# When stored sets give back their slots, and where a new set's square is issued, in a fused two-layer convolution kernel

## The chip, the cores and the metric

The kernel runs on one core of a Trainium2 chip. The metric is the device time of one execution in microseconds (us), lower is better. Before the change, three runs took 9905.83, 9907.52 and 9934.52 us; their median, 9907.52 us, is the time before.

## The reference, cut to what matters

The input x has 8 elements of 8 channels of 512 x 512, all float32. Layer 0 adds a small spectral convolution to x. Layer 1 takes the group-normalised result (called `xn` in the kernel) and runs three parts on it:

```python
drive = grid = x                       # a coupled map lattice, 15 steps
for _ in range(15):
    mapped = 3.9 * grid * (1.0 - grid)
    local = conv3x3_per_channel(mapped, K_local)
    physics = 0.7 * mapped + 0.3 * local
    grid = 0.85 * physics + 0.15 * drive
cml_out = clip(grid, 0.0001, 0.9999)
h = relu(conv3x3(x, Wp) + bp)          # 8 -> 128 channels
nca_out = sigmoid(conv1x1(h, Wu) + bu) # 128 -> 8
gin = concat([x, cml_out, nca_out])
g = sigmoid(conv1x1(relu(conv3x3(gin, Wg1))))
out = x + g * cml_out + (1 - g) * nca_out
```

The change touches the book-keeping of the lattice part alone. It does not change what is computed.

## The kernel before, in words

**The work.** Every element goes through four kinds of work, and one instruction stream per engine mixes them by hand: the lattice (`Half`, `convolve`, `settle`), the hidden convolution (`Hidden`: matmuls at L636, relus at L642 on ScalarE and L644 on VectorE, the 1x1 convolution at L655), the gate of the element before (`Gate`, L706 and L723), and the spectral layer of the element after (`layer0`: L305, L313, L363, L401 with its copy `ty` at L405, L433).

**The lattice.** Each element has two halves of four channels (`first`, `second`). A half is cut into five sets, k = 0 to 4, each four slabs of 32 rows. A set needs three tiles of 128 x 4 x 512: `dE` and `dO`, the drive for the even and the odd steps, loaded from `xn` by four DMAs of 256 KB each (L494), and `m`, the state. The first state is the square of `dE` minus a half: a MEMSET of two border columns on GpSimd (L515) and one ACTIVATE on ScalarE (L516), both in `square(k)`. A set's step is 48 matmuls in float32 (L536; the profile shows 96 records), two VectorE operations that take the result out of PSUM and add the drive (L591), and two squares on ScalarE (L597). A drive is scaled on GpSimd in `drive` (L529).

**The order.** A *tick* (`work`, L892) does two set-steps, A then B. An element has 75 ticks: ticks 0 to 37 hold the first half's 75 set-steps and the first one of the second half (tick 37 is A = first half, k = 4, step 15, and B = second half, k = 0, step 1), ticks 38 to 74 the rest. Step 15 of the first half is in ticks 35 (k = 0, 1), 36 (k = 2, 3) and 37 (k = 4); that of the second half is in ticks 72 (B, k = 0), 73 (k = 1, 2) and 74 (k = 3, 4). I call ticks 35 to 39 the *middle turn* (eight of them, one in each element) and ticks 72 to 76 the *end turn* (seven: ticks 75 and 76 are ticks 0 and 1 of the next element). In a tick, every engine gets its instructions in this order: the drives that are due (`prepare`), convolve A, convolve B with A's `settle`, the loads (`transfers`, which calls `others.feed` and then `fetch`), up to two rounds of the hidden convolution with their relus, the rest of B's `settle`, `squares()` (L906), then gate or spectral work and the 1x1 convolution, whose result gets its sigmoid on ScalarE every second time (L668), then `tick()` (L915), which issues what was put off to the end of this tick: the stores and the exchange of border rows (`renew`). All the DMAs named here are issued on SyncE's queue (SP), which handles them one after the other.

**The slots.** The tiles of sets live in a pool of 15 slots, `sets`, handed out first in, first out: `take` pops the oldest free slot, `drop` appends one. A half holds all 15 until its step 14. Then `settle` drops `dE` at step 14 and `dO` at step 15 (L603), and `m` after its store: `leave` (L568) clips the state on VectorE (L571) and puts off to the end of the tick a function that issues four DMAs to `cml` (L577) and drops the slot (L581). The half that comes next takes them: `fetch` (L509) loads its drives in the order (k, dE), (k, dO) for k = 0 to 4 as long as a slot is free, in each tick from eleven set-steps ahead on; `squares(n)` (L504) makes the state of set k in the tick in which k - 2 is n or n + 1, n being the half's own count, which makes it the tick before the set's first step. So `square` asks for a slot without asking whether one is free; and a slot that is handed out while its last user's store is still under way makes its new user wait for that store.

Of the kernel before, what the change touches and what calls it, by code (L numbers as in the profile page):

```python
# [128 lines left out]
def conv_layers(ctx: ExitStack, tc: tile.TileContext, a, out):  # L129
# [27 lines left out]
    sets, shared = Slots("set", 15), Slots("shared", SHARED)  # L157
# [12 lines left out]
    def later(ticks, work):  # L170
        put_off.append((now[0] + ticks, work))

    def tick(end=False):
        now[0] += 1
        due = [w for at, w in put_off if end or at <= now[0]]
        put_off[:] = [] if end else [(at, w) for at, w in put_off if at > now[0]]
        for work in due:
            work()
# [296 lines left out]
    class Half:  # L475
# [27 lines left out]

        def squares(self, n):  # L504
            for k in range(SETS):
                if k - 2 in (n, n + 1):
                    self.square(k)

        def fetch(self, n):  # L509
# [21 lines left out]
    def convolve(m, c0, step, ps):  # L531
        for n, dx in enumerate((1, 0, 2)):
            for t in range(4):
                for h in range(4):
                    at = slice(32 * h, 32 * h + 32)
                    nc.tensor.matmul(  # L536
                        ps[h // 2][32 * t : 32 * t + 32, h % 2],
                        band[at, c0 + (t if step % 2 else h), dx],
                        m[at, t, dx : dx + N],
                        start=(n == 0), stop=(n == 2), tile_position=(32 * h, 32 * t),  # L540
                    )
# [26 lines left out]
    def leave(m, k, half):  # L568

        g = m[:, :, 1 : N + 1]  # L570
        nc.vector.tensor_scalar(g, g, 0.0001, 1.0 - 0.0001, ALU.max, ALU.min)  # L571

        def store():
            for h in range(4):
                s = 4 * k + h
                lo, hi = SHARES[s]
                nc.sync.dma_start(  # L577
                    out=half.cml[1 + STARTS[s] + lo : 1 + STARTS[s] + hi, half.c0 : half.c0 + 4],
                    in_=g[32 * h + lo : 32 * h + hi],
                )  # L580
            sets.drop(m)  # L581

        later(1, store)

    def settle(half, step, k, ps):

        m, d = half.m[k], half.d[k, step % 2]
        u = m[:, :, 1 : N + 1]
        for q in range(2):
            at = slice(2 * q, 2 * q + 2)  # L590
            nc.vector.scalar_tensor_tensor(  # L591
                u[:, at], ps[q], FLOOR, d[:, at], ALU.max, ALU.add
            )
            if q:
                yield
            if step < STEPS:
                nc.scalar.square(u[:, at], u[:, at])  # L597
        if step == 1:
            half.drive(k, 0)
        elif step == STEPS - 2:  # L600
            nc.gpsimd.tensor_scalar(d, d, 0.5, None, ALU.add)  # L601
        elif step >= STEPS - 1:
            sets.drop(d)  # L603
        if step == STEPS:
            leave(m, k, half)
        elif (step - k) % HALO == 0:
            later(1, lambda: renew(half.m, k, step))
# [284 lines left out]
    def work(sets, rounds, e, after, transfers, squares=lambda: None):  # L892

        settled = iter(())
        for (half, step, k), ps in zip(sets, (pairs[:2], pairs[2:])):
            convolve(half.m[k], half.c0, step - 1, ps)
            next(settled, None)
            settled = settle(half, step, k, ps)
            next(settled)
            others.finish()  # L900
        others.finish()
        transfers()
        for ps in (pairs[:2], pairs[2:])[:rounds]:
            e.hidden.round(ps, after, settled)
        next(settled, None)
        squares()  # L906

        a, b, c, d = (pairs[i] for i in ((0, 1, 3, 2), (2, 0, 3, 2))[rounds == 1])

        point = rounds and e.hidden.n % 2 == 0  # L910
        others.first([a, b if point else c])
        if point:
            e.hidden.point(c[:, 0])
        others.second([d if point else c])
        tick()  # L915

    elements = [e]
    for n in range(-FIRST_ROUNDS, 0, 2):
# [2 lines left out]
    for b in range(B):  # L921
# [6 lines left out]
        for t in range(TICKS):  # L928
            assert not after or t < TICKS - 5 or not after.pieces
            halves = [(e.first, 2 * t), (e.second, 2 * t - TICKS)]  # L930
            if after:
                halves.append((after.first, 2 * t - 2 * TICKS))
            for half, n in halves:
                half.prepare(n)

            def squares():
                for half, n in halves:
                    half.squares(n)

            def transfers():  # L940
                others.feed(t)
                for half, n in halves:
                    half.fetch(n)

            now_sets = []
            for n in (2 * t, 2 * t + 1):
                half = (e.first, e.second)[n // TICKS]
                now_sets.append((half, n % TICKS // SETS + 1, n % SETS))

            more = done + (t + 1) * (rounds - done) // TICKS - e.hidden.n  # L950
            work(now_sets, min(more, 2 - e.hidden.n % 2), e, after and after.hidden, transfers, squares)
# [66 lines left out]
```

## Time and profile before

| what | value |
|---|---|
| median of three runs | 9907.52 us |
| the profiled execution's own time | 9903.73 us |
| its span, first to last instruction | 9901.9 us |
| around the span | 1.8 us |
| mean granted TensorE clock | 0.988 |
| TensorE (PE) busy | 9355.4 us, 94% of the span |
| VectorE (DVE) busy | 5876.2 us, 59% |
| ScalarE (ACT) busy | 4301.9 us, 43% |
| GpSimd (POOL) busy | 1762.5 us, 18% |
| DMA packets of the data queue q1 | 51.3% of 16 engines' span |

The trace is one profiled execution. A row of a timeline reads: start in us from the span's start, duration, engine, line, operation, what it writes and reads, how many were merged into the row, and in brackets how long the engine was idle before it and what ended that. "PEld" is the weight load. "issue" as a releaser means that no wait explains the idle time. A row of the waits reads: engine and line that waited, what it waited for, then us in total, times, longest. Several such waits may pass at once on different engines, and only those that TensorE feels at 94% busy can move the end of the kernel.

Where TensorE's lattice matmuls (L536) are counted off in groups of 192, a group begins each tick; in that way ticks are placed in the trace below.

### The profile page before, as it was taken

What the parts mean: (1) busy time and instruction counts of PE and PEld (TensorE: products, weight loads), DVE (VectorE), ACT (ScalarE), POOL (GpSimd) and SP (SyncE); (2) the same over time, 40 slices, a digit from 0 to 9 for tenths busy, and PEclk for the clock granted to TensorE, in tenths of its full rate; (3) what the DMA queues carried; (4) which work ended last, traced back from release to release, by engine and by line L of the source; (5) the groups of instructions that cost most, each with busy time, mean ns of one, the idle gap of its engine ahead of it and who ended that gap; (6) DMA issues with size and microseconds to landing.
All of it is one profiled execution on the core that took longest, in us unless ns stands there. A gap on an engine that the chain in (4) does not pass through costs nothing. (4 is left out here: it accounts for less than half of the span.)

```text
span 9901.9 us, 353033 instructions
## 1 busy us (share of the span) xinstructions
PE 9355.4 (94%) x160496; PEld 4299.0 (43%) x160496; DVE 5876.2 (59%) x6067; ACT 4301.9 (43%) x4445; POOL 1762.5 (18%) x1406
## 2 busy tenths in 40 slices
PE   6999999999999999999999999999999999898999
PEld 3444444444444434444344444444434444444433
DVE  5665555665566655666556655566555665555655
ACT  2544444443444434444444444445444454344423
POOL 2010111103121131111312013120221202221212
PEclk9999999999999999999999999999999999999999
DMA  5241355446544465445655356652665525753688
GB/s 152 86 121 34 80 141 135 138 126 167 139 129 142 129 162 138 133 128 136 163 140 143 117 141 162 145 157 94 148 164 139 161 97 142 171 124 95 147 200 202
DMA packets 625130, 1353.61 MB, mean 137 GB/s; under 512 B 72570, under 2 KB 72698, under 8 KB 593618
## 3 DMA queue, kind: packets, MB, share of 16 engines
q1 hardware_dynamic: 621280, 1329.89, 51.3%
q8 instruction: 1261, 20.66, 0.9%
q14 instruction: 235, 1.93, 0.1%
q10 hardware_dynamic: 2354, 1.14, 0.0%
HBM read 992.42 MB, written 268.78 MB: 127 GB/s over the span
## 5 line engine op out<-in xcount | busy, mean ns | idle before, releaser
L536 PE MATMUL pair<-m,band 32*32 32x512 f32 x115200 | 4093.8, 605 | 212.5 <-issue 99.6
L597 ACT ACTIVATE m<-m 128x1024 f32<-128x1024 f32 x2240 | 2363.7, 1055 | 2812.8 <-DVE m L591 2685.0
L536 PEld LDWEIGHTS pair<-m,band 32*32 32x32 f32 x115200 | 2258.3, 103 | 1955.8 <-issue 983.1
L636 PE MATMUL pair<-cols,w_p 32*128 32x511 f32 (+1 forms) x24576 | 2862.1, 603 | 47.0 <-issue 15.9
L591 DVE SCALAR_TENSOR_TENSOR m<-pair,dO 128x1024 f32<-128x1024 f32 x1280 | 1506.5, 1219 | 1384.6 <-PE pair L536 1214.6
L636 PEld LDWEIGHTS pair<-cols,w_p 32*128 32x128 f32 x24576 | 1275.9, 186 | 1645.0 <-issue 1116.1
L591 DVE SCALAR_TENSOR_TENSOR m<-pair,dE 128x1024 f32<-128x1024 f32 x1120 | 1318.8, 1219 | 1075.4 <-PE pair L536 870.9
L644 DVE TENSOR_SCALAR h<-pair,b_p 128x1024 f32<-128x1024 f32 x1024 | 1313.0, 1283 | 812.1 <-PE pair L636 803.3
L642 ACT ACTIVATE h<-pair,b_p 128x1024 f32<-128x1024 f32 x1024 | 1141.4, 1115 | 1044.1 <-PE pair L636 1043.9
L655 PE MATMUL pair<-h,w_u 128*32 128x512 f32 x8192 | 995.0, 598 | 136.2 <-DVE h L644 124.7
L729 POOL TENSOR_TENSOR mix<-mix 96x512 f32<-96x512 f32 x344 | 438.0, 1273 | 3809.0 <-ACT mix L727 3598.7
L706 PE MATMUL pair<-gin,w_g 128*32 128x511 f32 (+1 forms) x8256 | 965.9, 601 | 31.1 <-DMA gin<-nca 17.0
L711 POOL TENSOR_TENSOR mix<-mix 96x512 f32<-96x512 f32 x344 | 446.9, 1299 | 2006.1 <-DMA mix<-nca 1276.1
L601 POOL TENSOR_SCALAR dO<-dO 128x2048 f32<-128x2048 f32 x80 | 431.9, 5411 | 1228.5 <-DVE m L591 1228.5
L655 PEld LDWEIGHTS pair<-h,w_u 128*32 128x32 f32 x8192 | 249.0, 110 | 756.7 <-issue 384.7
L706 PEld LDWEIGHTS pair<-gin,w_g 128*32 128x32 f32 x8256 | 235.8, 110 | 711.3 <-issue 471.6
L668 ACT ACTIVATE y<-y,b_u 128x512 f32<-128x512 f32 x256 | 184.7, 721 | 808.5 <-DVE y L664 808.3
L734 DVE SCALAR_TENSOR_TENSOR mix<-mix,back 96x512 f32<-96x512 f32 x344 | 327.0, 951 | 147.3 <-POOL mix L729 147.3
L662 ACT COPY y<-pair 128x512 f32<-128x512 f32 x256 | 149.8, 585 | 599.8 <-PE pair L655 490.3
L716 DVE TENSOR_SCALAR mix<-pair,b_g 128x512 f32<-128x512 f32 x344 | 257.9, 750 | 247.8 <-PE pair L706 247.8
L723 PE MATMUL pair<-mix,w_g 128*32 128x512 f32 x2064 | 356.5, 593 | 10.5 <-DVE mix L716 8.5
L529 POOL TENSOR_SCALAR dO<-dO,base 128x512 f32<-128x512 f32 x320 | 238.6, 763 | 437.1 <-DMA dO<-xn 246.3
(86 smaller groups left out, 2661.4 us busy)
## 6 DMA issues: line engine op xcount, KB each, us to landing
gin<-xn SPq DMA_DIRECT2D x344, 384.0 KB
cols<-xn SPq DMA_DIRECT2D x256, 512.0 KB
x<-in_x SPq DMA_DIRECT2D x120, 1024.0 KB
gin<-cml SPq DMA_DIRECT2D x344, 320.0 KB
gin<-nca SPq DMA_DIRECT2D x344, 320.0 KB
dE<-xn SPq DMA_DIRECT2D x320, 256.0 KB
dO<-xn SPq DMA_DIRECT2D x320, 256.0 KB
mix<-xn SPq DMA_DIRECT2D x344, 192.0 KB
```

What stands on the lines that cost most here:

```text
L536: nc.tensor.matmul(ps[h // 2][32 * t : 32 * t + 32, h % 2], band[at, c0 + (t if step % 2 else h), dx], m[at, t, dx : dx + N], start=(n == ...
L591: nc.vector.scalar_tensor_tensor(u[:, at], ps[q], FLOOR, d[:, at], ALU.max, ALU.add)
L597: nc.scalar.square(u[:, at], u[:, at])
L601: nc.gpsimd.tensor_scalar(d, d, 0.5, None, ALU.add)
L636: nc.tensor.matmul(ps[g // 2][:, g % 2, lo:hi], w_p[p, dx, i % 2], self.cols[p, i // 2, at : at + hi - lo], start=(n == 0), stop=(n == 2), ...
L642: nc.scalar.activation(h[:, :2], ps[0], AF.Relu, bias=b_p)
L644: nc.vector.tensor_scalar(h[:, 2:], ps[1], b_p, 0.0, ALU.add, ALU.max)
L655: nc.tensor.matmul(ps[32 * g : 32 * g + 32], w_u[:, r % 4], h[:, g], start=(r == self.hs[0][0]), stop=(r == self.hs[-1][0]), tile_position ...
L706: nc.tensor.matmul(ps[32 * j : 32 * j + 32, lo:hi], gband[:, dx], gin[:, j, at : at + hi - lo], start=(n == 0), stop=(n == 2), tile_positi ...
L711: nc.gpsimd.tensor_tensor(d, d, ng, ALU.subtract)
L723: nc.tensor.matmul(ps[at], gpoint[:, at], mix[:, 3], start=True, stop=True, tile_position=(0, 32 * j),)
L729: nc.gpsimd.tensor_tensor(d, d, mix[: GR * C, 2], ALU.mult)
```

## The change

`leave` no longer drops the slot of a stored state in the function that issues the stores; that function puts the drop off once more, to the end of the next tick. `squares` makes a set's square only if it is not there yet and if a slot is free. And `work` calls `squares()` a second time at its very end, behind `tick()`. So what found no slot behind the relus is made at the tick's end, after the slots whose turn has come were given back.

```diff
@@ -503,7 +503,7 @@
 
         def squares(self, n):
             for k in range(SETS):
-                if k - 2 in (n, n + 1):
+                if k - 2 in (n, n + 1) and k not in self.m and sets.free:
                     self.square(k)
 
@@ -578,7 +578,7 @@
                     out=half.cml[1 + STARTS[s] + lo : 1 + STARTS[s] + hi, half.c0 : half.c0 + 4],
                     in_=g[32 * h + lo : 32 * h + hi],
                 )
-            sets.drop(m)
+            later(1, lambda: sets.drop(m))
 
         later(1, store)
 
@@ -913,6 +913,7 @@
             e.hidden.point(c[:, 0])
         others.second([d if point else c])
         tick()
+        squares()
 
     elements = [e]
```

## The prediction

> **What bounds the kernel now.** I read the shares first: TensorE is busy for 94% of the span, so only what TensorE waits for can pay. Then the waits of all engines (engine and line, what it waited for; us in total, times, longest):
>
> ```profile
> POOL m L515 <- DMA cml<-m: 197.7, 28, 17.9
> ...
> PEld pair L536 <- ACT m L516: 103.2, 38, 12.7
> PE pair L536 <- issue: 99.6, 59, 4.9
> ...
> PE pair L536 <- ACT m L516: 69.7, 21, 11.8
> ```
>
> GpSimd's MEMSET of a new state waits 198 us for stores out of the slot, and the lattice matmuls wait 69.7 us for squares (the weight loads' 103.2 us are mostly the same moments). These are upper ends. So third, the timeline at every turn. Middle turn of element 1, end of tick 37 and begin of 38, GpSimd, ScalarE and TensorE (three answers):
>
> ```profile
> 1853.07 0.11 POOL L515 MEMSET m<- 128x8 f32 x1 [17.44 <-DMA cml<-m]
> 1855.60 0.11 POOL L515 MEMSET m<- 128x8 f32 x1 [2.42 <-DMA cml<-m]
> ```
> ```profile
> 1848.71 1.11 ACT L642 ACTIVATE h<-pair,b_p 128x1024 f32<-128x1024 f32 x1 [0.51 <-PE pair L636]
> 1853.21 2.00 ACT L516 ACTIVATE m<-dE,mhalf 128x2048 f32<-128x2048 f32 x1 [3.39 <-POOL m L515]
> 1855.74 2.00 ACT L516 ACTIVATE m<-dE,mhalf 128x2048 f32<-128x2048 f32 x1 [0.52 <-POOL m L515]
> 1857.65 0.56 ACT L405 COPY ty<-pair 128x512 f32<-128x512 f32 x1
> 1858.11 0.72 ACT L668 ACTIVATE y<-y,b_u 128x512 f32<-128x512 f32 x1
> ```
> ```profile
> 1850.44 1.92 PE L655 MATMUL pair<-h,w_u 128*32 128x512 f32 x16
> 1855.27 1.92 PE L536 MATMUL pair<-m,band 32*32 32x512 f32 x4 [2.90 <-ACT m L516]
> 1858.26 8.05 PE L536 MATMUL pair<-m,band 32*32 32x512 f32 x188 [1.08 <-ACT ty L405]
> ```
>
> ScalarE is ready at 1849.82, sits 3.39 us behind a store, and does both squares ahead of `ty`, whose bank convolve A needs: TensorE is done at 1852.36, its lattice matmuls run from 1858.26. The two convolutions then take 8.05 us where 192 matmuls take 6.58 in the ticks around: the granted clock is 0.50 for 6.83 us from 1854.7.
>
> The end turn looks different (elements 3 to 4, ScalarE then TensorE):
>
> ```profile
> 4868.71 3.88 ACT L516 ACTIVATE m<-dE,mhalf 128x2048 f32<-128x2048 f32 x2
> 4872.65 0.72 ACT L668 ACTIVATE y<-y,b_u 128x512 f32<-128x512 f32 x1
> ...
> 4884.46 1.05 ACT L597 ACTIVATE m<-m 128x1024 f32<-128x1024 f32 x1
> 4885.40 3.88 ACT L516 ACTIVATE m<-dE,mhalf 128x2048 f32<-128x2048 f32 x2
> ```
> ```profile
> 4887.44 8.91 PE L536 MATMUL pair<-m,band 32*32 32x512 f32 x192 [4.04 <-ACT m L516]
> ```
>
> Here ScalarE goes from L597 to the squares without a pause: no store holds it, the tick simply has one hidden round to cover them. The seven end turns have about 28 us of this wait and 13 us of one of 1.6 us and more a tick later, 42 of the 69.7. They stay.
>
> **Slots, counted by hand.** Middle turn, free list before: tick 36 loads (3,dE) to (4,dO) into the slots of dO1, m0, m1, dO2; set 0's state gets dO3; in tick 37 sets 1 and 2 get m2 and m3, whose eight stores were issued at the end of 36; in 38 sets 3 and 4 get dO4 and m4. After: tick 36 has only dO1 and dO2 to load into, so (4,dE) and (4,dO) come in tick 37, into m0 and m1; set 1 gets dO4 behind the relus, set 2 finds nothing and gets m2 at the end of 37; set 3 gets m3 behind the relus of 38, set 4 gets m4 at its end. End turn, after: (3,dO) moves from tick 73 to 74; set 0 gets dO4 behind the relus of 74, set 1 m1 at its end; set 2 m2 behind those of 75, set 3 m3 at its end; set 4 m4 in 76. So 30 of the 80 squares come at a tick's end, and no instruction is added.
>
> **Middle turns, what goes.** TensorE's end of L655 against the start of the 188 matmuls, then the convolutions' excess over 6.54 us: element 1: 5.9 + 1.5. Element 2: 3063.79 - 3060.85 = 2.9, + 1.2. Elements 3, 4, 5: 1.6, 1.8, 1.8, where no store is late and only `ty` lies behind two squares. Element 6: 3.8 + 1.6. Element 7 (no next element, few rounds): 8983.24 - 8971.48 = 11.8, + 2.4 (9.01 us at half clock). Element 0: 0.3. In sum 29.9 + 6.7 = 36.6 us.
>
> **Middle turns, what comes.** Set 1's square follows the relu at once (1849.8 to 1851.8 in element 1), `ty` is done at 1852.4, A starts as TensorE gets free. Set 2's square now stands behind the sigmoid, which waits for VectorE's y: about 1853.4, 1854.1, square until 1856.1. B is due 3.3 us (half of 6.58) after A, at 1855.7: a wait of 0.4. The same sum gives 0.2, 0.4, 0.5, 0.2, 0.3, 0.3, 0.4 for elements 0 to 6, 2.3 together. Element 7: A waits until set 1's square ends at 8972.1 (0.6), and set 4's square at the end of 38 now meets m4's stores, issued until 8983.8, before landing; with the 4.5 us from issue to release that element 1 shows, 8988.3, square until 8990.3 against 8988.7: 1.6.
>
> No row of before shows a square at a tick's end. Below: a gain, since `ty` and y come sooner. Above: the whole 2.0 us at each of 15 covers (middle 37, end 74), 30 us, should VectorE's y be late. I take the 0.2 to 0.5, by the nearest row: the sigmoid at 4872.65, right behind y. Queued behind that square are the next tick's squares L597, due 3.5 us later, and behind its MEMSET the next drive; both have room.
>
> **Code stalls.** The rows "issue" are gaps of 1 to 4 us in ticks 35 to 37 and 71 to 75, while loads and stores stream (element 4, 2.92 us ending at 5475.19). The only reader left is the code queue, q8, 16 KiB packets. Loads and stores are neither more nor fewer after, they are spread otherwise, so I keep these gaps. But where TensorE stood and code came meanwhile, it will now meet it: element 2's packet landed at 3067.9 with 0.16 us of stall after 2.9 us of standing; I take 3.0 off there, 0.7 in element 1, 1.0 in element 7. The Trainium skill (Runtime: NRT & Kernel Launch, Instruction fetch mechanics) holds that crossing a 16 KiB block is mostly hidden; by it these 4.7 us stay a gain, and the 99.6 us above would not be there. I go by the rows.
>
> A rule that speaks against the change: DMA: Bandwidth & Descriptors, Anatomy of one DMA, gives a fixed 2.0 us and bytes / 436 GB/s (fitted to GpSimd's path). For 208 KB that is an estimated 2.5 us. Set 1's four stores end their issue near 1847.2 (half of this row, SP):
>
> ```profile
> 1843.16 7.97 SPq L577 DMA_DIRECT2D cml<-m  x8
> ```
>
> They would be in at 1849.7, just as ScalarE gets free, and only `ty`'s 1.5 us would be there to win; so too in elements 2 and 6, and in element 7 the wait would be 7.2 instead of 11.8. By the rule the change is worth some 17 us less, 8 in all (9899). The trace releases the MEMSET at 1853.07, 5.9 us after the issue, and the measurement decides.
>
> **End turns.** In tick 74 set 1's square goes behind the sigmoid: 4873.4 to 4875.4, B due at 4875.1: 0.3 lost, seven times, 2.1 us. In 75 set 2's square stands where it stood, set 3's follows with nothing between: 0. The four DMAs of (3,dO) pass the stores of m1 and m2 on SP. GpSimd has the drive of (3,dO) ahead of set 2's MEMSET (4874.90 before, needed by 4885.40), and between them lie 3.8 us of that drive and 4.2 of two others: it may land until 4877.4 at no cost. By the nearest row, (4,dE) issued at 4862.94 from the same place on SP, and 6 us to land, it is in by 4871. I take 0; its upper end is rival 3. Likewise (4,dE), (4,dO), eight DMAs a tick later, pass m2's and m3's stores; their first reader is the square at the end of 38, over 10 us on: 0.
>
> **Sum.** Middle turns 36.6 - 2.3 - 0.6 - 1.6 - 4.7 = 27.4 (by element 0.1, 6.3, 0.6, 1.4, 1.5, 1.5, 5.0, 11.0), less 2.1 in the end turns: 25.3 us. The profiled execution, 9901.9 in its span and 1.8 around, would be 9878.4. It lies 3.8 under the median, and I take the difference off the median: 9907.5 - 25.3 = 9882.
>
> **Rivals.** (1) *The burst flattens.* Tick 36 loses 8 of 16 loads; if code then comes in time, tick 37's gaps (1.0, 2.0, 2.9, 2.8, 0.9 = 9.6 us) and some 8 us of half clock behind them go too: 43 us, 9864. For: they stand only in these streams. Against: SP issues back to back until the same moment. (2) *The wait becomes a code stall.* Starting 3 to 6 us earlier into the stream, elements 1, 2, 6 and 7 lose 3 us each and half a clock window (1.7): 19 less, minus the 4.7 booked: 11 us remain, 9896. For: element 2. Against: element 6's packets come 3.6 us after they are due, the calm value. (3) *Slower: (3,dO) holds GpSimd.* If it lands after 4877.4, some 14 us from its issue, set 2's MEMSET in tick 75 is late, ScalarE stands with the next tick's L597 behind it, and TensorE with both. At 23 us from the issue (GpSimd's longest wait for such a load, L529 on `dO<-xn`, is 27.0) that is 8 to 9 us in each of seven end turns, 59 - 25: 9941. Against: loads of tick 74 are issued four in 1.8 us, where in the dense stretches they take 3.6. (4) *It doesn't do what it says:* only if slots were free anyway; the count has 30 squares moved. Under 1%, in (2).
>
> **How the numbers follow.** My forecast 0.58, (1) 0.17, (2) 0.18, (3) 0.07. A measurement of this kernel tells about 0.3%, 30 us, from no change, so faster means under 9877.8. The forecast's own range is 9868 to 9893 (the covers from gain to 1 us each, code from 0 to 9); 0.25 of its 0.58 lies past the bound. Faster 0.25 + 0.17 = 0.42; same 0.33 + 0.18 = 0.51; slower 0.07. The range takes in (1) and (2): 9860 to 9904.
>
> **What would show it.** Right: MEMSET's wait for `cml` well under 100 us; `ty` ahead of the second square in tick 37; convolve A of 38 right behind L655, element 7's 11.8 us gone; L516's hold on TensorE still at 50 to 65 us, nearly all in end turns. Wrong: new "issue" rows in tick 38; a square at a tick's end that ends over 1 us after B is due; a MEMSET in tick 75 behind L529.

## The result, and the profile after

The median of 19 runs after is 9888.22 us (9869.14 to 9914.17), that of 19 runs before beside them 9912.2 us. The medians lie 24.0 us apart; the ratio, by which all runs here are compared, is 0.9981, with an interval of 0.9974 to 0.9988: about 19 us less (12 to 26), inside the 0.3% that were called no change. The prediction was 25.3 us less. The same kernel run a second time, beside other runs of before (`e13_after_again`), gave 0.9987 (0.9981 to 0.9994), about 13 us less (6 to 19).

The profiled execution of after is not one of its better ones: 9904.16 us, 16 above its own median, so that its span (9902.4 us) equals that of before (9901.9). What differs must therefore be read stretch by stretch. First the waits (engine and line, what it waited for; us in total, times, longest), the rows that were shown of before, and one more:

```profile
POOL dO L529 <- DMA dO<-xn: 338.9, 32, 26.9
...
PE pair L536 <- issue: 111.9, 65, 4.7
...
PEld pair L536 <- ACT m L516: 98.9, 52, 6.4
...
PE pair L536 <- ACT m L516: 56.3, 23, 5.5
POOL m L515 <- DMA cml<-m: 55.8, 12, 9.7
```

The MEMSET's wait for stores fell from 197.7 to 55.8 us, and TensorE's for squares from 69.7 to 56.3, its longest from 11.8 to 5.5. TensorE's "issue" row at L536 grew from 99.6 to 111.9. The sum held 4.7 of these 12.3 us: the first sign of something that it did not hold.

The middle turn of element 1, GpSimd, then ScalarE, then TensorE (start, duration, engine, line, operation, idle time before and what ended it):

```profile
1844.28 1.20 POOL L515 MEMSET m<- 128x8 f32 x2 [7.10 <-DVE m L591]
```
```profile
1850.86 1.11 ACT L642 ACTIVATE h<-pair,b_p 128x1024 f32<-128x1024 f32 x1 [0.51 <-PE pair L636]
1851.88 1.99 ACT L516 ACTIVATE m<-dE,mhalf 128x2048 f32<-128x2048 f32 x1
1853.77 0.58 ACT L405 COPY ty<-pair 128x512 f32<-128x512 f32 x1
1855.31 0.72 ACT L668 ACTIVATE y<-y,b_u 128x512 f32<-128x512 f32 x1 [0.97 <-DVE y L664]
1855.94 1.99 ACT L516 ACTIVATE m<-dE,mhalf 128x2048 f32<-128x2048 f32 x1
```
```profile
1852.60 1.92 PE L655 MATMUL pair<-h,w_u 128*32 128x512 f32 x16
1854.45 6.93 PE L536 MATMUL pair<-m,band 32*32 32x512 f32 x192
```

The MEMSETs no longer wait for a store. The first square follows the relu without a pause, `ty` stands between the two squares, and the 192 matmuls begin where L655 ends. They take 6.93 us, where 6.58 was the undisturbed value: convolve B begins 0.05 us behind the end of the second square and loses 0.35 to it (0.4 was expected). Before, the convolutions took 8.05 us there and began 5.9 us behind L655.

The end turn, elements 3 to 4, ScalarE and TensorE, as it was expected to look:

```profile
4854.45 1.99 ACT L516 ACTIVATE m<-dE,mhalf 128x2048 f32<-128x2048 f32 x1
...
4857.64 0.72 ACT L668 ACTIVATE y<-y,b_u 128x512 f32<-128x512 f32 x1 [1.19 <-DVE y L664]
4858.26 1.99 ACT L516 ACTIVATE m<-dE,mhalf 128x2048 f32<-128x2048 f32 x1
```
```profile
4865.95 3.87 PE L536 MATMUL pair<-m,band 32*32 32x512 f32 x39 [3.37 <-issue]
...
4877.51 8.08 PE L536 MATMUL pair<-m,band 32*32 32x512 f32 x192 [4.04 <-ACT m L516]
...
4892.41 4.10 PE L536 MATMUL pair<-m,band 32*32 32x512 f32 x116 [1.55 <-ACT m L516]
```

The square of set 1 has moved behind the sigmoid. The waits of 4.04 and 1.55 us are still there; before has the first in the row that the prediction shows, and the second here:

```profile
4903.17 6.58 PE L536 MATMUL pair<-m,band 32*32 32x512 f32 x192 [1.55 <-ACT m L516]
```

The gap of 3.37 us ("issue") is a stall without a wait; in before it was 1.23 us at that place. What such gaps are, the traces show. Count TensorE's records, weight loads and matmuls together, in blocks of 256. Of the 69 gaps of 0.3 us and more in before, 67 stand at the same place of a block, behind its 192nd record (120.4 of their 122.7 us), and each of these ends 1.2 to 1.8 us after a packet of 16 KiB has landed on q8, a moment that makes up 8% of the time. After has 71 of 73 gaps at that place, and no kernel here has more than three elsewhere. q8 brings 1261 packets for 322,931 records, one for each 256. So these gaps are TensorE waiting for its own code, and all kernels below have the same edges at the same matmuls.

To see where the time went I cut each trace at the first lattice matmul of every tick and summed the lengths of the ticks over all elements. "Middle" is ticks 33 to 40, "end" is 70 to 74 with 0 to 2, "gate" is 3 to 24 with 53 to 69 (ticks where the gate and the spectral work go on, and in which the change moves no instruction), "rest" is all else. Differences of one profiled execution each to before's, in us; the last column is the "issue" idle time of TensorE in the gate ticks, gaps of 0.3 us and more (before: 21.3):

| kernel | middle | end | gate | rest | span | issue in gate ticks |
|---|---|---|---|---|---|---|
| after | -28.5 | +5.7 | +19.5 | +3.6 | +0.5 | 29.4 |
| after again | -33.7 | -5.1 | +16.5 | +2.5 | -19.8 | 36.4 |
| middle only | -29.0 | +0.9 | -3.5 | +1.8 | -29.9 | 28.5 |
| end only | -1.9 | -0.8 | +16.0 | +3.4 | +16.7 | 36.2 |
| end only again | +0.5 | -2.3 | +19.2 | +10.8 | +28.3 | 35.7 |
| end, both moves | +7.0 | -0.6 | -2.9 | -4.2 | -0.6 | 24.4 |
| end, squares | +0.1 | +0.6 | -7.7 | +5.1 | -1.8 | 23.0 |
| end, loads | +2.5 | +3.9 | -0.8 | -0.2 | +5.5 | 28.6 |
| hold loads | -22.4 | +5.8 | +4.2 | +6.0 | -6.4 | 30.3 |
| all at end | +27.1 | +32.0 | -22.3 | +6.9 | +43.7 | 16.4 |
| ahead | -26.7 | -32.2 | +33.8 | +8.3 | -16.9 | 42.9 |
| ahead, middle | -35.6 | -36.5 | -0.1 | +3.1 | -69.0 | 23.7 |
| stores twice | +157.3 | +121.1 | +2.1 | +17.3 | +297.9 | 30.8 |

The middle turns gained what the prediction said, or some us more, and the end turns lost a little in one profile and gained as much in the other. But ticks in which nothing was moved took 16 to 20 us more. That is the time that is missing. The sum repeats, its places do not: of the 19.5 us of after, 13.5 lie in element 7 and 3.9 in element 6; in the second profile these two have -2.0 and 0.1, and elements 1, 2 and 5 have 17.3.

### The profile page after: what moved, and what is told of

It is laid out like the page before. It is cut to its first block, busy times and chain, and to the rows that moved or that the text cites. A ratio compares the mean times of both kernels' runs of the same rounds, so it can differ in the third digit from the quotient of the medians.

```text
span 9902.4 us, 353135 instructions
## 1 busy us (share of the span) xinstructions
PE 9365.5 (95%) x160496; PEld 4294.7 (43%) x160496; DVE 5872.5 (59%) x6067; ACT 4303.2 (43%) x4445; POOL 1769.8 (18%) x1406
## 3 DMA queue, kind: packets, MB, share of 16 engines
q8 instruction: 1261, 20.66, 0.9%
## 5 line engine op out<-in xcount | busy, mean ns | idle before, releaser
L536 PE MATMUL pair<-m,band 32*32 32x512 f32 x115200 | 4091.7, 604 | 205.1 <-issue 111.9
L536 PEld LDWEIGHTS pair<-m,band 32*32 32x32 f32 x115200 | 2247.3, 103 | 1948.3 <-issue 992.9
L655 PE MATMUL pair<-h,w_u 128*32 128x512 f32 x8192 | 993.0, 597 | 136.2 <-DVE h L644 123.1
L706 PE MATMUL pair<-gin,w_g 128*32 128x511 f32 (+1 forms) x8256 | 972.6, 604 | 36.5 <-DMA gin<-nca 20.9
L655 PEld LDWEIGHTS pair<-h,w_u 128*32 128x32 f32 x8192 | 249.3, 110 | 756.8 <-issue 384.8
L668 ACT ACTIVATE y<-y,b_u 128x512 f32<-128x512 f32 x256 | 184.8, 722 | 828.1 <-DVE y L664 828.1
L529 POOL TENSOR_SCALAR dO<-dO,base 128x512 f32<-128x512 f32 x320 | 238.0, 762 | 489.4 <-DMA dO<-xn 338.9
```

The source lines that it names most:

```text
L536: nc.tensor.matmul(ps[h // 2][32 * t : 32 * t + 32, h % 2], band[at, c0 + (t if step % 2 else h), dx], m[at, t, dx : dx + N], start=(n == ...
L655: nc.tensor.matmul(ps[32 * g : 32 * g + 32], w_u[:, r % 4], h[:, g], start=(r == self.hs[0][0]), stop=(r == self.hs[-1][0]), tile_position ...
L706: nc.tensor.matmul(ps[32 * j : 32 * j + 32, lo:hi], gband[:, dx], gin[:, j, at : at + hi - lo], start=(n == 0), stop=(n == 2), tile_positi ...
```

## The experiments

**The theories.** The first: the whole gain comes from giving back the first half's states later (middle turn), and doing the same with the second half's (end turn) only costs. Its rivals: the gain is one of the loads alone, which leave their slots to the squares; or the second call of `squares` alone does it; or the two turns only work together. For the cost in the gate ticks: it comes with a square at a tick's end, or with the load moved, or with the order of both, or with the later give-back itself, that is other slots and other waits. An interval of these ratios is some 6 to 20 us wide on either side, so the ratio judges the whole and the table says where. Before and most kernels have one profile each, so a single number of the table can be off by some us: the two pairs of repeats differ by up to 11.

**Only the first half's states later.** In the second half, and so in the end turn, the slot is given back as before.

```diff
-            later(1, lambda: sets.drop(m))
+            later(1, lambda: sets.drop(m)) if half.c0 == 0 else sets.drop(m)
```

> The later drop for states of the first half alone, so only middle turns change; end turns keep the early drop and find slots behind the relus as before. My theory (middle turns win by 27.4 us, end turns lose 2.1 by the square behind the sigmoid and perhaps more by the loads moved into tick 74): 27 us less than before, so 3 to 6 us less than the full change. Rival (end turns gain because the loads are spread): 10 to 20 us less than before, worse than the full change.

Measured: 9869.53 us, ratio 0.9967 (0.9954 to 0.9979), about 32 us less than before. Half the change does at least as much as all of it: the interval touches that of after (0.9974 to 0.9988) and lies clear of that of its repeat (0.9981 to 0.9994). Its middle turns gain 29.0 us, its gate ticks stay near where they were (-3.5). So the two turns need not work together.

**Only the second half's.** The condition turned round.

```diff
-            later(1, lambda: sets.drop(m))
+            later(1, lambda: sets.drop(m)) if half.c0 else sets.drop(m)
```

> The later drop for states of the second half alone, so only end turns change. My theory: 2 to 6 us more than before, with longer code gaps (issue) in tick 75 and shorter ones in ticks 73 and 74. Rival (spreading pays): 5 to 10 us less than before.

> The end-only kernel once more, unchanged, for a second profile and other runs. If its 23 us belong to the program: again 15 to 30 us above before, and again more code gaps in the gate ticks (3 to 24 and 53 to 69; 36 us of gaps there against 21 in the profile of before). If they belonged to those runs: within 8 us of before.

Measured: 9926.68 us, 1.0023 (1.0014 to 1.0033), and again beside other runs of before 9933.2 us, 1.0025 (1.0016 to 1.0034): 23 to 25 us slower. The sign was as expected; the expected 2 to 6 us were four to twelve times too small. The end turns themselves did not get longer (-0.8 and -2.3); the gate ticks did (+16.0 and +19.2), both times. With -33 in the middle and +23 here the sum is near the -19 and -13 of the whole, inside the intervals: the two halves of the change add. "End only" also has the second call of `squares`, and its middle turns are as before (-1.9 and +0.5): the call alone gains nothing there.

**Before, with two loads of the middle turn held a tick.** No square and no give-back is moved; `(4,dE)` and `(4,dO)` of the second half wait from tick 36 to 37, and leave their slots to the squares.

```diff
         def fetch(self, n):
-            while n >= -11 and self.loads and (self.loads[0][2] or sets.free):
+            hold = 8 if self.c0 and n < -1 else 0
+            while n >= -11 and len(self.loads) > hold and (self.loads[0][2] or sets.free):
```

> The kernel before, but in the middle turn the eight loads of set 4 are held back from tick 36 to tick 37; slots are given back early and both squares stay behind the relus. If the middle turn's store wait comes of eight loads standing ahead of the stores on SP (my theory), the MEMSET waits in tick 37 nearly vanish here too, only the order of ty behind two squares stays (1.6 to 1.8 us in elements 1 to 6, 10 us together): 15 to 18 us less than before. If it comes of the slot being too young, whatever stands on the queue (rival): under 6 us less.

Measured: 9903.23 us, 0.9999 (0.9991 to 1.0007): nothing. The profile shows both a hit and a miss. Rows of GpSimd and TensorE (in this kernel L516, L517 and L537 are before's L515, L516 and L536):

```profile
POOL m L516 <- DMA cml<-m: 178.9, 29, 11.9
...
PE pair L537 <- issue: 122.5, 66, 4.3
...
PE pair L537 <- ACT m L517: 64.9, 21, 6.1
```

The hit: the 11.8 us of element 7 are gone and the middle turns are 22.4 us shorter, four fifths of the change's 28.5, so most of what the middle turns gain goes with the loads that leave their slots to the squares. The miss: MEMSET's waits for stores, expected to nearly vanish in tick 37, only fell from 121.8 to 75.5 us there, and in tick 38 they grew from 15.0 to 43.9; what vanished is the part that TensorE felt (in tick 38 from 15.0 to 3.3). And 16 us came back in the end turns, the gate ticks and the rest, the "issue" row grew by 23 us, and the runs show no gain at all. Here, too, time shifted outside the edited place.

**Before, with all squares at the tick's end.** The call of `squares` stands only behind `tick()`.

```diff
-        squares()
...
         tick()
+        squares()
```

> The kernel before with early drops, but every square is made at the tick's end and none behind the relus. It prices the cover that the change keeps for the first square of a tick. Theory: convolve A waits for a whole square each time: 3.6 us in ticks 74 to 75 of seven end turns and 1.8 more than now in middle turns of elements 3 to 5, store waits in the others unchanged or 2 us shorter: 25 to 35 us more than before. Rival (the place of a square matters little, the slot does): within 8 us of before.

Measured: 9954.67 us, 1.0059 (1.0045 to 1.0073), 58 us slower, more than the 25 to 35 expected. Three rows of the waits:

```profile
PE pair L536 <- ACT m L516: 146.5, 41, 12.1
POOL m L515 <- DMA cml<-m: 144.0, 23, 15.9
...
PE pair L536 <- issue: 98.7, 56, 4.7
```

TensorE's wait for squares doubles (69.7 to 146.5). So a square at the tick's end is not free as such: two in a row stand behind the sigmoid, convolve A waits for the first (3.45 us in the end turn of elements 3 to 4), and the two convolutions then take 8.03 us instead of 6.58. The change is cheap because the first square keeps its place. Here the gate ticks took 22 us less, so the sign of that shift is not bound to the later call.

**Before, with one part of the end turn's order each, and both.** The slots are given back as before; only the squares of sets 1 and 3 go to the tick's end, or only the load of `(3,dO)` waits from tick 73 to 74, or both.

```diff
-                if k - 2 in (n, n + 1):
+                if k - 2 in (n, n + 1) and end == (self.c0 == 0 and k in (1, 3)):
```
```diff
-            while n >= -11 and self.loads and (self.loads[0][2] or sets.free):
+            hold = 12 if not self.c0 and n == -4 else 0
+            while n >= -11 and len(self.loads) > hold and (self.loads[0][2] or sets.free):
```

> The kernel before, with early drops and all loads where they were; only the squares of sets 1 and 3 in the end turn are made at the tick's end. It is one half of the change in the end turn, by itself. My sum says 2.1 us more than before (0.3 us under convolve B, seven times), and 0 to 5 is still in line with it. If the square at the tick's end is what the end turn pays for (rival): 15 us more or above.

> The kernel before, with early drops and both squares behind the relus; only the four loads of (3,dO) in the end turn are held from tick 73 to tick 74, behind the stores. It is the other half. The later drop for the second half alone took about 23 us more than before; if the moved loads and the code gaps that come with them in tick 75 carry that, this one takes 12 to 23 us more. If not (rival: the places of squares, or something outside the turn): within 6 us of before.

> Early drops, with both moves in the end turn: the loads of (3,dO) held to tick 74 and the squares of sets 1 and 3 at the tick's end. It has the order of the end-only kernel on every queue, but other slots for the states. Each move alone was within 0.1% of before, the end-only kernel 23 us above it. If the two moves together cost this (theory A): 15 us or more above before. If it comes with the later drop itself, by other slots and other waits (theory B): within 8 us of before.

Measured: squares 9905.32 us, 0.9998 (0.9989 to 1.0006); loads 9902.0 us, 0.9998 (0.9988 to 1.0007); both 9905.19 us, 1.0001 (0.9993 to 1.0009). None of them costs anything that can be told. The kernel with both moves issues the end turn's squares and loads in the order of "end only": in the two traces all engines have the same work in the same order, but for one sigmoid in the first tick. Yet the repeat of "end only", run beside it, was 24 us slower. What is left between them is what the give-back itself decides: which slot each tile gets, and which waits follow. SyncE has 9437 records in the traces of after and "end only", 9448 in before, "middle only" and "end, both moves", and the difference lies in the end ticks: there before has 331 records that are no DMA, after 320 and "end only" 321. In the gate ticks each engine has as many records without work in these traces as in before, to within four.

The gate ticks 3 to 24 of element 7 show the difference at its plainest. TensorE's "issue" row at L536 (L537) in that window: first "both moves" (298.7 us for these 22 ticks), then "end only" (307.5), then its repeat (305.7). Before has 295.7 us, and 3.4 in this row; after has 304.0, its repeat again 298.7.

```profile
PE pair L537 <- issue: 7.9, 4, 3.7
```
```profile
PE pair L536 <- issue: 10.8, 4, 4.0
```
```profile
PE pair L536 <- issue: 8.9, 5, 4.0
```

The row tells only part of it, 1.0 and 2.9 of the 7 to 9 us between them. Over all gate ticks "end only" has 36.2 us of "issue" against 24.4 of "both moves", 11.8 of the 18.9 us between them: 25 waits for code against 15.

Something else in these ticks tells the kernels apart, the DMA packets. The row of the data queue on the page, of before, after, "end only" and "both moves" (packets, MB, share of 16 engines' span):

```profile
q1 hardware_dynamic: 621280, 1329.89, 51.3%
q1 hardware_dynamic: 621280, 1329.89, 52.8%
q1 hardware_dynamic: 621280, 1329.89, 52.7%
q1 hardware_dynamic: 621280, 1329.89, 51.3%
```

The same packets take longer. In the gate ticks the mean packet of 2 KiB (some 289,000) takes 136.6 to 137.3 ns in all six profiles with the later give-back in the end turn ("stores twice" and "ahead" among them), and 130.4 to 131.2 in seven without it; "hold loads", where slots change hands in another way in the middle turn, stands between with 133.9. In the gate ticks of each of elements 1 to 7 it is so, one by one. So what the give-back decides goes with how long packets of other tiles take, hundreds of us later. That the longer packets are what makes the code late is not shown: "stores twice" has them, and its gate ticks are at +2.1.

**After, with squares made ahead.** At the tick's end, once all drives are on their way, `squares` may also make those that are due a tick later, if a slot is free.

```diff
-        def squares(self, n):
+        def squares(self, n, end):
+            ahead = 2 if end and not self.loads else 0
             for k in range(SETS):
-                if k - 2 in (n, n + 1) and k not in self.m and sets.free:
+                if n <= k - 2 < n + 2 + ahead and k not in self.m and sets.free:
```

> The changed kernel, whose call at the tick's end may also make the squares that are due in the next tick, once all drives are loaded and if a slot is free. In the end turn set 2's square then comes at the end of 74 and set 4's at the end of 75, in the middle turn set 3's at the end of 37. By the profile TensorE stands 4.0 us at the begin of tick 76 and 1.6 at that of 77 in each of seven end turns: 39 us; 0.7 of each 4.0 stay as convolve B's wait for set 3. Theory: 25 to 35 us less than the changed kernel, about 45 to 55 less than before. Rival (ScalarE's next L597 is late instead): within 10 us of the changed kernel.

Measured: 9876.49 us, 0.9964 (0.995 to 0.9978), by the ratios 17 us less than after, where 25 to 35 were expected. The end turns give 38 us (from +5.7 to -32.2), about all of the 39 that TensorE stood there. But tick 77 alone lost 23.0 us, and the gate ticks are at +33.8.

**The two that paid, together.** Later give-back for the first half only, and one square ahead.

```diff
+            ahead = 1 if end and not self.loads else 0
...
-            later(1, lambda: sets.drop(m))
+            later(1, lambda: sets.drop(m)) if half.c0 == 0 else sets.drop(m)
```

> The later drop for the first half's states alone, the early one for the second half's, and the tick's end may make one square ahead, of the next set in turn, when all drives are loaded. Loads of the end turn stay in tick 73, sets 2 and 4 get their squares a tick early. Theory: the middle-only kernel's 31 us less than before and most of the 39 us that TensorE stands at ticks 76 and 77: 55 to 65 us less than before. Rival: the early squares push the next L597, 30 to 40 less.

Measured: 9844.54 us, 0.994 (0.9921 to 0.996), about 60 us less than before (40 to 78), as expected, and faster than before and after. The end turn of elements 3 to 4, ScalarE and TensorE (all lines one higher than after's):

```profile
4835.31 3.90 ACT L517 ACTIVATE m<-dE,mhalf 128x2048 f32<-128x2048 f32 x2
4839.09 0.72 ACT L669 ACTIVATE y<-y,b_u 128x512 f32<-128x512 f32 x1
4839.71 2.00 ACT L517 ACTIVATE m<-dE,mhalf 128x2048 f32<-128x2048 f32 x1
...
4851.63 3.89 ACT L517 ACTIVATE m<-dE,mhalf 128x2048 f32<-128x2048 f32 x2
```
```profile
4844.70 2.15 PE L537 MATMUL pair<-m,band 32*32 32x512 f32 x41 [1.63 <-issue]
...
4850.93 6.68 PE L537 MATMUL pair<-m,band 32*32 32x512 f32 x192 [1.29 <-ACT h L643]
...
4862.81 3.62 PE L537 MATMUL pair<-m,band 32*32 32x512 f32 x100
```

The third square comes a tick early, right behind the sigmoid, and the 192 matmuls that waited 4.04 us and then took 8.08 now wait 1.29 for a relu and take 6.68. The wait of 1.55 a tick later is gone too. Over the seven end turns, ticks 75 and 76 are 27.6 and 22.1 us shorter; tick 77 gave 19.8 back.

**After, with every finished state stored twice.** Each of the four stores is issued two times, which adds data and nothing else; the question was whether the "issue" gaps grow with what streams.

```diff
-            for h in range(4):
+            for h in (*range(4), *range(4)):
```

> The changed kernel, which stores every finished state twice to the same place: eight more DMAs in each tick of step 15, no other work. It tests that TensorE's gaps without a wait (issue) in the turns come of data that streams while its code is fetched. If so: gaps in the turns up by half or more (from about 100 us in sum), 50 to 120 us more time. If the gaps come of something else (rival): gaps within 15 us, and what time it takes more is in waits for stores and loads.

Measured: 10201.87 us, 1.0301 (1.0285 to 1.0316), 298 us slower.

```profile
PE pair L536 <- ACT m L516: 307.9, 40, 18.9
...
POOL m L515 <- DMA cml<-m: 248.7, 28, 22.5
...
PE pair L536 <- issue: 107.6, 62, 5.3
```

The gaps did not grow (111.9 to 107.6). All of it is the old wait again: MEMSET behind stores, TensorE behind squares. It does not settle whether more data means more gaps, because TensorE now stands 251.6 us longer behind squares, and code can come in that time. It does show the change's limit: with stores twice as long, one tick more is not enough.

**After again.** The same kernel once more, run beside the repeat of "end only" and "both moves".

> The changed kernel once more, for a second profile: its first profiled execution was 16 us over its own median. By the middle-only and the end-only kernel: 8 to 25 us less than before; the middle turns in the profile again 25 to 31 us shorter than before, and the code gaps in the gate ticks tell how much of the rest is theirs.

Measured: 9894.77 us, 0.9987 (0.9981 to 0.9994). The gate ticks are at +16.5 us again, with 36.4 us of "issue" in them: the sum belongs to the kernel and not to the one execution, though it lies in other elements.

## Why the prediction was right in its turns and short in its sum

**The middle turns: right, in mechanism and size.** Predicted by element 0.1, 6.3, 0.6, 1.4, 1.5, 1.5, 5.0, 11.0, together 27.4 us; measured 1.3, 6.5, 1.7, 1.1, 2.4, 1.8, 5.3, 8.5, together 28.5 (33.7 in the second profile, where element 3 has 3.7 and element 7 has 9.7). The squares and loads moved as the slots counted by hand had it, `ty` went ahead of the second square, and convolve B lost the 0.3 to 0.4 us that the nearest row (L668, then a square) had promised. TensorE's time at half the granted clock in the middle turns fell from 92.2 to 75.1 us, which is the second part of the gain: where TensorE stands less, it also loses less clock.

The measurement also decides the rule of the Trainium skill on what a store takes (DMA: Bandwidth & Descriptors, Anatomy of one DMA). By it the gain in these turns would have been some 17 us less, 10 of the 28.5 measured; the releases as the trace has them gave the 28.5.

Element 7 was 2.5 us short of its 11.0. TensorE there, first the two rows of before, then after:

```profile
8983.24 9.01 PE L536 MATMUL pair<-m,band 32*32 32x512 f32 x192 [11.76 <-ACT m L516]
8997.70 8.61 PE L536 MATMUL pair<-m,band 32*32 32x512 f32 x192 [5.45 <-ACT m L516]
```

```profile
8974.62 5.40 PE L536 MATMUL pair<-m,band 32*32 32x512 f32 x147 [1.55 <-ACT m L516]
8982.51 2.18 PE L536 MATMUL pair<-m,band 32*32 32x512 f32 x45 [2.49 <-issue]
...
8990.14 8.70 PE L536 MATMUL pair<-m,band 32*32 32x512 f32 x192 [5.45 <-ACT m L516]
```

A waited 1.55 us instead of 0.6, the gap that had been hidden under the old wait came out at 2.49 instead of 1.0, and the 1.6 booked for set 4 did not come: the 5.45 in the last row stood there before. The three together make 0.8 of the 2.5; the rest is not traced.

**The gaps without a wait: right on the whole, wrong by place.** I kept them and took 4.7 us for those that standing had hidden. In tick 38 they rose from nothing to 7.4 us, so that rival 2 held for part; in tick 37 they fell from 11.5 to 1.4, so that rival 1 held for part; ticks 35 and 36 went from 15.1 to 18.6 and from 21.8 to 20.8. Over the middle turns it is 48.4 before, 48.8 after and 47.6 in the second profile, over the end turns 50.6, 52.9 and 46.5. Spreading the loads moved the gaps and took none away that can be told. That these gaps are code, as the prediction argued from what was left, is shown by their places in the stream.

**The end turns: right in place, too small to be told in size.** 2.1 us of loss were predicted; ticks 70 to 77 of elements 0 to 6 show 3.8 (and 4.0 of gain in the second profile), with 15 us less in ticks 70 to 74 and 15.3 more in tick 75. L516's hold on TensorE is 56.3 us, in the expected 50 to 65. Rival 3, the slow one, did not come: GpSimd's wait for `dO` grew from what before has here to 338.9 us in all, its longest stayed, and TensorE's wait for squares did not grow with it. Rival 4 fell with the first row of MEMSET.

```profile
POOL dO L529 <- DMA dO<-xn: 246.3, 20, 27.0
```

**The step that failed is one that was not there.** The sum booked nothing outside the turns, as no instruction is moved there. With the later give-back in the end turn the gate ticks took 16.0 to 19.5 us more in all four profiles of "after" and "end only"; without it, in six kernels of the same family ("middle only", "both moves", "squares", "loads", "hold loads", "ahead, middle"), -7.7 to +4.2; with squares ahead and both halves given back later it was +33.8, with all squares at the end, and slots given back as before, -22.3. So the end turn's part did not cost the 2.1 us booked but 23 to 25 us when made alone, and about 14 to 20 on top of the middle part (0.9967 to 0.9981 and 0.9987). In "end only" the added waits for code account for 14.9 of the 16.0 us; in after they account for 8.1, and 17.1 us more at half clock, each of which loses half, for about 8.5; in its repeat they are 15.1 and 1.7, against 16.5. They are not the whole account: "middle only", "loads", "hold loads" and "stores twice" have 28.5 to 30.8 us of them, as much as after, and no such cost, as other waits or half clock went down there.

The total came near all the same: 9888 us lies in the forecast's own range, and the 25.3 us at the edge of the first interval, but outside that of the repeat. That is in part luck: in its second set of runs the same kernel gained 13 us, half of the forecast.

Shown are the kind of ticks, the size, that it comes with the give-back and not with the order of squares and loads, and that DMA packets take some 6 ns longer in those ticks whenever the end turn gives back later. Not shown is the cause. Other slots mean other addresses; how these make packets longer, and whether longer packets make the code late, was not tried. The eleven waits less on SyncE lie in the end ticks, so they are no direct cause elsewhere. "Stores twice" speaks against a fixed link: it has the later give-back in both halves and the longer packets, and its gate ticks show +2.1.

## What to carry to other kernels

In this kernel giving back a buffer later helped where the next user would meet a store still under way, and not in the other turn: apply it to the one turn alone, and let what does not find a slot come later without moving the first one. Then look at what TensorE still waits for in the next tick: making one square ahead brought about 27 us on top of the middle part, more than the whole change. And in a kernel whose TensorE is busy for 94% of the span, a sum over the edited ticks can be right to a us or two and the total still be 20 us off, so compare the traces tick by tick, and take the total from many runs.

## What the runs showed of the hardware that I had not expected

- TensorE's gaps without a wait are its code: all but one to three of each kernel's (67 of 69 in before, 120.4 us) stand at the same place of a block of 256 of its records, and end some 1.2 to 1.8 us after a 16 KiB packet of q8 has landed.
- Their sum stayed about the same in the edited turns when the loads were only spread: 48.4 and 48.8 us in the middle turns, 50.6 and 52.9 in the end turns. Where TensorE stood less in one tick, they came in the next; in "ahead, middle", where it stands less, they rose to 65.2 us in the end turns.
- Twice the stores did not raise that sum (111.9 to 107.6 us), while the whole took 298 us longer.
- When buffers are given back in one place goes with how long DMA packets take in others: 2 KiB packets of the gate ticks took 137 ns in six profiles with the later give-back in the end turn, 131 in seven without it.
- Two kernels with the same TensorE stream and the same order of squares and loads in the end turn, different in slots and waits, lie 24 us apart (1.0001 and 1.0025, intervals that do not touch), most of it in ticks where they have the same work (+16.0 and +19.2 against -2.9).
- One execution differs from the next by up to 45 us (9869 to 9914 in 19 runs of after), so that a single profile can hide a gain of 19 us.
